# Pinning the first layer's TensorE instructions to program order, with other lengths of filler work in each step

## The chip, the cores and the metric

The kernel runs on one core of one Trainium2 chip. The time is device microseconds of one execution; a figure for a kernel is the median of its runs. The profile is of one execution. In it PE is TensorE (matmuls), PEld its weight loads, DVE is VectorE, ACT ScalarE, POOL GpSimd and SP SyncE; L100 is line 100 of the kernel before.

## What is computed

A trunk of two layers on x of shape (4, 512, 512), all in float32. The diff touches the first layer only. Cut to what matters:

```python
x  = L0_attn_hidden_states                  # (4, 512, 512)
xn = _layernorm(x)
x  = x + _L0_attn_ref(xn, ...) + _L0_ffn_ref(xn, ...)     # layer 0
xn = _layernorm(x)
x  = x + _L1_attn_ref(xn, ...) + _L1_ffn_ref(xn, ...)     # layer 1

# layer 0, attention: 32 heads of 16, a scan over NM = 32 mini-batches of K = 16 tokens
def step(carry, x):
    W1_s, b1_s = carry
    xq, xk, xv, eta_mb = x
    Z1 = xk @ W1_s + b1_s
    grad = _ln_fused_l2_bwd(Z1, xv - xk, ln_w, ln_b)
    Attn1 = jnp.tril(xq @ xk.swapaxes(-1, -2))
    b1_bar = b1_s - jnp.tril(eta_mb) @ grad
    Z1_bar = xq @ W1_s - eta_mb * Attn1 @ grad + b1_bar
    last_eta = eta_mb[:, :, -1, :, None]
    W1_new = W1_s - (last_eta * xk).swapaxes(-1, -2) @ grad
    b1_new = b1_s - jnp.sum(last_eta * grad, axis=-2, keepdims=True)
    out = xq + _ln(Z1_bar, ln_w, ln_b)
    return ((W1_new, b1_new), out)
# then: out = _ln(out, post_norm_weight, post_norm_bias) @ o_w.T

# layer 0, feed-forward: 512 -> 1408 -> 512
g = xf @ gate_w.T * gate_s;  u = xf @ up_w.T * up_s
out = (silu(g) * u) @ down_w.T * down_s
```

Every step of the scan needs the state that the step before it wrote, so the 32 steps come one after the other. The feed-forward part and the projections don't depend on the scan. Layer 1 is an attention with 16 heads and a feed-forward part with 4 experts.

## The kernel before

**Chunks.** Layer 0's 512 positions are cut into NCHUNK = 8 chunks of CH = 4 steps. A chunk has 4 batches of 64 tokens, CW = 256 columns.

**The step** (main loop of the scan, state in PSUM tiles `wacc`, `pz`, `pso`). `weights_out(n)` copies the state `wacc` to SBUF, as the block-diagonal operand `wq_bd` (DVE and ACT, L312) and as `wh` (ACT, L315). `first_product` is a matmul of 512 columns with `gsum` and 32 small matmuls `pz <- wq_bd, sk`. `queries_out` starts `pso` with 16 small matmuls from `wh`. `gradient` (L333 to L371) is a chain of vector operations on DVE with two on ACT, from `pz` to `grad`. `out_operands` makes `gh` (POOL, L401) and `a_bd` (DVE, L404). `update` copies `grad` into the block-diagonal `g_bd` (two copies on DVE, two on ACT, L375) and adds 16 small matmuls `wacc <- g_bd, km`; DVE adds to `gsum` (L386). `emit_out` adds 16 small matmuls to `pso` from `gh` and `a_bd` and DVE copies the result to `zch`; at the end of a chunk it is stored to DRAM and loaded back in another layout as `zb` (L434, L436). `prepare(n+1)` loads `kv` (L287) and makes `sk`, the second half of `wq_bd` and `km` on POOL (L294, L296, L301).

**The other work.** All that doesn't belong to the scan is written as Python generators that yield at certain points with a cost in microseconds. `between(ch)` chains them for a chunk: 11 slices of `gate_up` (8 matmuls of 256 columns into `pf`, with weights `wg`, `wu` loaded on SP; cost 3.43), the post-norm and output projection `finish(ch-1)` of the chunk that the scan has left, the `down` product into `pd`, a `value_bias` for layer 1, and what the next chunk of the scan needs: `norm_turn`, `keys`, `token_tile`, `queries`. `finish` runs, between its yields: a square on ACT (`pn_sq`, L543), two matmuls of 512 columns with `ones16`, for each a root on ACT and a reciprocal on DVE (`pn_rs`, L549 and L550), a product on DVE (L551), a scale and bias on ACT (L553) and an addition on POOL (L556), all on `zb`; then four matmuls of `onesd` and `zb`, a subtraction on DVE (L561) and a square on ACT (L562); then eight matmuls of one column, and for two halves four matmuls with `wo`, an update of `yf` on DVE (L576), a store, and a row norm; then transposes. Its first part is drawn in `between` behind the gate_up slice NI - 3 = 8, the others behind the parts of `down`. In the last chunk, finish(6) is drawn whole ahead of `down`.

**How they are mixed.** `fill(us)` draws from the chain of all generators until their costs have used up the time allowed; a debt is carried over in `due`. The main loop calls it three times in a step, with the three lengths of GAPS (L37): behind the step's gradient and operands, between `update` and `emit_out`, and behind `emit_out`. LAST_GAPS is for the last chunk, LAST_FINISH for the last finish.

**What sets the order on an engine.** The program is given to a scheduler[...]; it may move one past another where no dependency forbids it. `tc.keep_in_program_order` around an instruction holds it to the order in which the program issues it, among the instructions of its engine that are held so. Before, only three products at the end of layer 1 and the loads of its expert weights are held. Every matmul of layer 0 but a few goes through `mm` (L99); transposes are issued in `transposed` (L124) and `token_tile` (L234). `psum()` gives the PSUM tiles `pj`, of which there are two, as of `pf`.

## Time and profile before

| what | value |
|---|---|
| median of 3 runs | 2203.81 us (2200.7 to 2208.69) |
| the profiled execution's own time | 2204.35 us |
| its span in the profile | 2202.6 us |
| mean granted TensorE clock | 0.986 |
| layer 0 (to the last of its matmuls) | 0 to 1047 us |
| transition (PE waits for the load of `xe`) | 15.86 us |
| matmuls of one gate_up slice, PE | 3.45 us |
| pz with its gsum matmul; first half of pso; wacc; second half of pso, PE | 1.44; 1.19; 0.58; 0.61 us |
| one matmul into pd | 0.86 us |
| `pn_sq` pair; four `onesd <- zb`, PE | 1.98; 1.98 us |
| reciprocal of `pn_rs`, DVE | 3.35 us |
| addition to `zb`, POOL | 2.34 us |

A row of the timeline has the start in us from the start of the span, the duration, the engine, the line and operation, output and inputs with their shapes, how many instructions the row joins, and in brackets the idle time of the engine ahead of it with what ended it. Time that an engine is idle costs something only where that engine carries the work that sets the end.

### The profile page before, as it was taken

The numbers are of one execution on the slowest core, as the hardware profiler recorded it, in microseconds if no ns is written. First come the engines' busy times: TensorE is split into PE (matmuls) and PEld (weight loads), VectorE is DVE, ScalarE is ACT, GpSimd is POOL, SyncE is SP. The second block draws the span as 40 slices with busy tenths as digits, with TensorE's granted clock in tenths as the row PEclk, the third lists the DMA queues.
The fourth block names the chain that finished last, engine by engine and source line by source line (L and its number), as shares of the span: only waits on it lengthen the run. The fifth ranks groups of instructions, "written<-read, shape, count | busy, mean of one in ns | idle before, by whom it ended". The sixth has DMA issues, their size and how long they took to land.

```text
span 2202.6 us, 29431 instructions
## 1 busy us (share of the span) xinstructions
PE 2101.9 (95%) x10194; PEld 1195.0 (54%) x10194; DVE 1164.2 (53%) x2320; ACT 868.4 (39%) x1793; POOL 493.8 (22%) x540
## 2 busy tenths in 40 slices
PE   8999999999999999999799989999999999999999
PEld 6767586757667676745344444444444444444444
DVE  5445655455645554732011256666566656666663
ACT  2334353333433342423101255545454455455552
POOL 5232332233322332410010111111111111111110
PEclk9999999999999999999899889999999999999999
DMA  6555554546354556543830232333333323333332
GB/s 179 165 139 151 140 164 131 170 116 181 106 162 137 140 159 173 169 134 112 308 114 0 86 100 61 75 95 75 83 77 96 77 69 74 76 74 76 94 95 76
DMA packets 287856, 259.29 MB, mean 118 GB/s; under 512 B 52955, under 2 KB 210844, under 8 KB 286684
## 3 DMA queue, kind: packets, MB, share of 16 engines
q1 hardware_dynamic: 275296, 251.72, 40.8%
q10 hardware_dynamic: 11500, 5.32, 0.9%
q8 instruction: 82, 1.34, 0.3%
q14 instruction: 66, 0.54, 0.1%
q0 software_dynamic: 912, 0.36, 0.1%
HBM read 161.60 MB, written 29.62 MB: 87 GB/s over the span
## 4 chain that ended last, share of the span: by engine, by line
PE 75%; DVE 10%; ACT 8%; DMA 2%; issue 2%; POOL 1%; SPq 0%; ACTq 0%; DVEq 0%; POOLq 0%
PE pj L100 15%; PE pf L100 11%; PE po L1059 10%; PE pc L1044 7%; PE sc L998 5%; PE pd L100 5%; PE pq L989 5%; ACT prob L1003 3%; PE epg L845 3%; PE epo L890 2%; PE epu L845 2%; ACT prob L1005 2%; PE pso L100 2%; PE pz L100 2%; PE pk L982 2%
## 5 line engine op out<-in xcount | busy, mean ns | idle before, releaser
L998 PE MATMUL sc<-kT,qT 96*128 96x512 f32 x512 | 235.7, 598 | 15.1 <-ACT prob L1003 13.4
L975 POOL TENSOR_TENSOR kT<-t_k,t_k 32x512 f32<-32x512 f32 x64 | 80.7, 1261 | 722.0 <-PE pq L989 403.7
L1003 ACT ACTIVATE prob<-sc,mx 128x512 f32<-128x512 f32 x256 | 173.1, 683 | 146.5 <-DVE mx L1000 146.4
L1059 PE MATMUL po<-vo,ctxT 128*128 128x512 f32 x512 | 223.0, 592 | 1.5 <-ACT ctxT L1049 1.5
L1044 PE MATMUL pc<-prT,lv 128*128 128x512 f32 x496 | 224.1, 594 | 0.0
L1013 DVE STREAM_TRANSPOSE tt<-prob 128x512 f32<-128x512 f32 x252 | 166.6, 697 | 60.5 <-ACT prob L1005 58.2
L989 PE MATMUL pq<-cq,uq 128*128 128x512 f32 x384 | 175.2, 592 | 0.0
L100 PE MATMUL pf<-xT,wg 128*128 128x256 f32 x704 | 170.7, 384 | 3.5 <-DVE hid L456 1.9
L1005 ACT ACTIVATE prob<-prob,sm 128x512 f32<-128x512 f32 x256 | 171.7, 724 | 3.6 <-DVE sm L1004 3.6
L998 PEld LDWEIGHTS sc<-kT,qT 96*128 96x128 f32 x512 | 95.9, 190 | 140.9 <-issue 110.9
L1000 DVE TENSOR_REDUCE mx<-sc 128x1 f32<-128x512 f32 x256 | 164.3, 681 | 7.1 <-PE sc L998 4.5
L100 PE MATMUL pf<-xT,wu 128*128 128x256 f32 x704 | 166.9, 380 | 1.1 <-DMA wu<-in_wu 1.1
L100 PE MATMUL pd<-wd,hid 128*128 128x512 f32 x352 | 164.7, 601 | 0.2 <-DMA wd<-in_wd 0.2
L1059 PEld LDWEIGHTS po<-vo,ctxT 128*128 128x128 f32 x512 | 97.0, 190 | 124.2 <-issue 116.7
L1044 PEld LDWEIGHTS pc<-prT,lv 128*128 128x128 f32 x496 | 94.6, 191 | 120.1 <-issue 112.0
L100 PEld LDWEIGHTS pf<-xT,wg 128*128 128x128 f32 x704 | 130.9, 190 | 30.5 <-DVE hid L456 6.1
L100 PEld LDWEIGHTS pf<-xT,wu 128*128 128x128 f32 x704 | 133.4, 190 | 20.8 <-DMA wu<-in_wu 1.9
L1069 DVE TENSOR_TENSOR y<-po,y 128x512 f32<-128x512 f32 x64 | 44.2, 691 | 152.6 <-PE po L1059 152.6
L989 PEld LDWEIGHTS pq<-cq,uq 128*128 128x128 f32 x384 | 73.0, 190 | 91.8 <-issue 87.3
L983 ACT ACTIVATE kT<-pk,b_UK 64x512 f32<-64x512 f32 x64 | 43.7, 683 | 197.0 <-PE pk L982 197.0
L456 DVE SCALAR_TENSOR_TENSOR hid<-pf,us,sg 128x256 f32<-128x256 f32 x88 | 41.6, 476 | 122.3 <-ACT sg L455 121.6
L100 PEld LDWEIGHTS pd<-wd,hid 128*128 128x128 f32 x352 | 63.3, 190 | 60.4 <-issue 52.6
(253 smaller groups left out, 3145.4 us busy)
## 6 DMA issues: line engine op xcount, KB each, us to landing
prT<-tt SPq DMA_DIRECT2D x1008, 64.0 KB, 2.1
wd<-in_wd SPq DMA_DIRECT2D x176, 256.0 KB, 2.9
wg<-in_wg SPq DMA_DIRECT2D x88, 256.0 KB, 3.4
wu<-in_wu SPq DMA_DIRECT2D x88, 256.0 KB, 2.9
rows<-rows SPq DMA_DIRECT2D x128, 66.0 KB, 2.2
kv<-rows SPq DMA_DIRECT2D x32, 264.0 KB, 4.6
gu<-in_gu SPq DMA_DIRECT2D x4, 2048.0 KB, 8.0
xt<-in_x SPq DMA_DIRECT2D x32, 128.0 KB, 3.2
```

Source lines behind the costliest of these rows:

```text
L100: nc.tensor.matmul(out, lhsT=lhsT, rhs=rhs, start=start, stop=stop, skip_group_check=True)
L845: nc.tensor.matmul(ps, lhsT=w[:, c, col : col + P], rhs=xe[:, :, c, e, :], start=(c == 0), stop=(c == NC - 1))
L975: nc.gpsimd.tensor_sub(t[RD:mid, :], t1[RD:mid, :], t2[RD:mid, :])
L989: nc.tensor.matmul(pq, lhsT=w["uq"][i][:, h, :], rhs=cq[:, i, b, :], start=(i == 0), stop=(i == nq - 1))
L998: nc.tensor.matmul(ps, lhsT=qT[:KQ, i * P : (i + 1) * P], rhs=kT[:KQ, :], start=True, stop=True)
L1000: nc.vector.tensor_reduce(mx, ps, AX.X, ALU.max, negate=True)
L1003: nc.scalar.activation(pr, ps, AF.Exp, bias=mx, scale=1.0, accum_out=sm)
L1005: nc.scalar.mul(pr, pr, sm)
L1013: nc.vector.transpose(out=tt[:, :, :, i, :], in_=pr.rearrange("p (kb e j) -> p kb e j", e=2, j=K))
L1044: ins = nc.tensor.matmul(pc, lhsT=lv[:, b, k, :], rhs=prT[:, k, :], start=(k == 0), stop=(k == E - 1))
L1059: ins = nc.tensor.matmul(po[e], lhsT=ctxT[:, h, e * P : (e + 1) * P], rhs=w["vo"][:, h, :], start=(h == 0), stop=(h == HPG - 1),)
L1069: nc.vector.tensor_add(y[b][:, e, :], po.pop(e), y[b][:, e, :])
```

## The change

Two things. The three lengths of filler in each step become 13, 4 and 6 instead of 11, 4 and 8 (in the last chunk 12, 4, 3 instead of 10, 4, 5): the sum stays. And the TensorE instructions issued by `mm`, `transposed` and the key transposes of `token_tile` are held to program order. Behind these lines the line numbers grow by 2.

```diff
-GAPS, LAST_GAPS = (11.0, 4.0, 8.0), (10.0, 4.0, 5.0)
+GAPS, LAST_GAPS = (13.0, 4.0, 6.0), (12.0, 4.0, 3.0)
...
         def mm(out, lhsT, rhs, start=True, stop=True):
-            nc.tensor.matmul(out, lhsT=lhsT, rhs=rhs, start=start, stop=stop, skip_group_check=True)
+            tc.keep_in_program_order(
+                nc.tensor.matmul(out, lhsT=lhsT, rhs=rhs, start=start, stop=stop, skip_group_check=True)
+            )
...
         def transposed(src):
             pt = psum().rearrange("p (c t) -> p c t", c=NC)
             for c in range(NC):
-                nc.tensor.transpose(pt[:, c, :], src[:, c * P : (c + 1) * P], ident)
+                tc.keep_in_program_order(nc.tensor.transpose(pt[:, c, :], src[:, c * P : (c + 1) * P], ident))
             return pt
...
             pk = psum()
             for be in range(NC):
-                nc.tensor.transpose(pk[:, be * P : (be + 1) * P], k1[ch][:, be, tcols], ident)
+                tc.keep_in_program_order(nc.tensor.transpose(pk[:, be * P : (be + 1) * P], k1[ch][:, be, tcols], ident))
```

## The prediction

> **What bounds the kernel now.** I read the page's engine row first, then the windows, then the waits of TensorE, then the timeline around single waits.

> ```profile
> PE 2101.9 (95%) x10194; PEld 1195.0 (54%) x10194; DVE 1164.2 (53%) x2320; ACT 868.4 (39%) x1793; POOL 493.8 (22%) x540
> ```

> TensorE (PE) is busy 95% of the span, DVE only 53%. The second view cuts out layer 0's scan, and inside it the first finish (columns: stretch, its length, busy time and count of PE, PEld, DVE, ACT, POOL, granted clock, DMA share, GB/s):

> ```profile
> 98.00:1047.00 949.00, 907.62 (x6997) 628.78 (x6989) 498.42 (x1087) 345.80 (x692) 273.32 (x336) 0.99 0.51 147
> 185.00:215.00 30.00, 27.25 (x214) 19.03 (x213) 19.27 (x34) 18.18 (x28) 10.39 (x14) 0.95 0.46 141
> ```

> 949 us for 31 steps is about 30 us a step (28.4 where no transition lies in between), while the dependent loop is short: from pz to the end of the g_bd copies 9.7 to 10.4 us undisturbed, wacc 0.6, 3 to 5 until wq_bd and wh are rewritten, so about 14. The scan is bound by the amount of PE work. The change neither adds nor removes a matmul, so only PE's waits can be won or lost. PE rows of 0 to 1047 us have 50.9 us of gaps over 0.25 us, 10.4 of them before 98 us. The waits by releaser (total, times, longest):

> ```profile
> PE pz L100 <- POOL wq_bd L296: 6.7, 3, 2.2
> PE pj L100 <- ACT pn_sq L543: 5.5, 4, 2.9
> PE pj L100 <- POOL zb L556: 5.0, 5, 2.1
> PE pso L100 <- POOL gh L401: 4.6, 4, 2.0
> PE wacc L100 <- ACT g_bd L375: 4.3, 3, 1.7
> ```

> Two families: the steps' own products (pz, pso, wacc), and the post-norm of finished chunks (pn_sq, zb).

> **What the pinning removes.** The two instruction orders differ: PE has 1489 rows of grouped instructions before and 1469 after, because groups that the scheduler had split (six matmuls of emit_out, then wacc, then the other ten) become whole. After, each step is pz, pso, about 13 us of filler, wacc, filler of 4, emit_out, filler of 6. Layer 1's PE order is unchanged. The steps' badly placed products were waits like these:

> ```profile
> 270.55 0.37 PE L100 MATMUL pso<-a_bd,gh 128*32 128x68 f32 x10 [1.98 <-POOL gh L401]
> 407.35 1.08 PE L100 MATMUL pz<-wq_bd,sk 128*32 128x128 f32 x32 [2.22 <-POOL wq_bd L296]
> ```

> Summed from the gap rows: gh 1.99 + 1.66 + 0.40, wq_bd 3 x 2.22, g_bd 0.29 + 1.17 = **12.2 us**. With 13 us plus pz/pso (2.63: pz with gsum 1.44, pso 1.19) ahead of wacc, 15.6 us cover the 10-us gradient, and 6 us ahead of the next pz cover the 3 to 5 for wq_bd. I take all 12.2 as gone (bounds: 0 if other waits replace them at the same places, 12.2).

> **What the longer first gap does.** The fill times per step are the same in sum (23, in the last chunk 19), so no work moves between steps; about 2 us move from behind emit_out to ahead of wacc. That costs nothing itself: wacc has 4 + 6 us of filler behind it. Its cover ends where a finish stretches the gradient: pz to g_bd took 15.9, 18.3, 16.6 and 15 us in steps 13, 17, 21, 25, where the two 3.35-us reciprocals of finish lie on DVE. There 15.6 us don't suffice by 1 to 3 us: counted below.

> **What the pinning adds.** Filler matmuls are pinned too. What waits in finish, until now passed by later down or feature matmuls, now stops PE, and everything behind it: the next gate_up, wacc, pz. First finish, before:

> ```profile
> 190.37 0.81 ACT L375 COPY g_bd<-grad 32x256 f32<-32x256 f32 x2 [4.85 <-DVE grad L370]
> 191.20 1.06 ACT L543 ACTIVATE pn_sq<-zb 128x1024 f32<-128x1024 f32 x1
> 192.31 1.98 PE L100 MATMUL pj<-pn_sq,ones 128*128 128x512 f32 x4 [0.68 <-ACT pn_sq L543]
> ...
> 209.55 2.34 POOL L556 TENSOR_TENSOR zb<-zb,q 128x1024 f32<-128x1024 f32 x1
> 211.95 3.56 PE L100 MATMUL pj<-zb,onesd 128*128 128x256 f32 x8 [2.07 <-POOL zb L556]
> ```

> ACT's square stands behind step 4's g_bd copies in both orders, so it is ready 10.9 us after step 4's pz (181.4 to 192.3). After, the first gap of step 4 has one gate_up (3.45) ahead of the pn_sq matmuls: PE arrives at 2.63 + 3.45 = 6.1, and waits **4.8**. From pn_sq to the end of zb on POOL took 18 to 19.6 us in most finishes (19.6, 17.8, 17.2, 19.0, none read, 18.4, 15.5 for finish 0 to 6); I take 18.4. After has 14.7 us of PE work between: **3.6** of wait. Together 8.4 against 2.74 before.

> The other finishes in the same way, by the PE work that the new order puts between (17.3, 16.8, 16.1, 14.1, 14.7, 12.7): finish 1 to 3, own chain less filler 0.5 + 0.4 + 2.9 plus about 1.2 for pn_sq, 5.0 against 3.0; finish 4, 3.3 for the late wacc of step 21 and 1.5 for zb, 4.8 against 4.7; finish 5, 18.4 - 14.7, 3.8 against 0.6; finish 6, which the last chunk draws in one go with nothing between, zb 3.9 (2.8 by its own chain, 5.7 by 18.4; nearer its own row), the second pn_sq 3.6, transposes behind the row norm 2.4: 9.9 against 2.6; finish 7, 6.4 against 7.1. Sum 38.3 against 20.7: **+17.6**. Floor: the chain's durations alone add to about 14 us (so +7); ceiling: every chain 19.6 and pn_sq always at 10.9 (so +30).

> Smaller: start-up 12.6 against 10.4 (the transposes of k and the bias chain no longer overtaken by gate_up) +2.2; the bo_part pairs of value_bias 6.9 against 4.8, +2.1; rest 1.6 against 2.7, -1.1. DMA: the same transfers on SP; weight loads are issued in the changed order but a buffer ahead, as before; wg's wait is in the rest.

> Sum without the clock: -12.2 + 17.6 + 2.2 + 2.1 - 1.1 = **+8.6 us**.

> [...]Fewer but longer gaps also touch TensorE's clock. Behind the 2.07-us gap above, the eight matmuls took 3.56 us where the same two fours take 1.98 elsewhere: +1.6, with 0.95 granted in 185 to 215. Gaps of 2.88 (at 987) and 2.69 (at 1036) cost +1.3 and +1.5, while 2.22-us gaps at 407, 527 and 650 cost nothing (clock 1.00). The long one shows the full price:

> ```profile
> 1062.55 5.16 PE L845 MATMUL epg<-xe,gu 128*128 128x512 f32 x8 [15.86 <-DMA xe<-xe_d]
> 1067.54 3.60 PE L845 MATMUL epu<-xe,gu 128*128 128x512 f32 x8
> ```

> 5.16 - 3.60 = 1.56. [...]here the trace decides that gaps of 2 to 3 us may do. [...]By the trace, seven or eight of about 3 us or more give about 11.5, less before's four (1.6 + 1.3 + 1.5, and 1.2 behind gaps of 1.72 and 0.56 at 697 to 700; 5.6): +6. I take **+4**, since three gaps of 2.2 show that one near the edge isn't sure to slow anything.

> 2204.35 (profiled execution; its span is 2202.6, and 1.75 around it stays) + 8.6 + 4 = **2217 us**, 0.6% more. It stands 0.5 above the median of 2203.81, well within the runs' 2200.7 to 2208.7.

> **Rivals.** *A, the other side: the finishes are covered.* If ACT's square runs ahead of step 4's gradient (zb had landed at 184.6, 3.2 after pz) and POOL adds zb at once, the 17.6 shrinks to about zero, the other +3.2 remains, the 12.2 is won, and with shorter gaps two of before's slow spells (1.5 each) go: 2204.35 - 12.2 + 3.2 - 3 = 2192. For it: the floor of 14 us for the chain is below most fillers. Against: the ACT order of after still has g_bd's copies first, and before's chains never came below 15.5. It decides if the pn_sq wait is under 1 us and the chain under 15.

> *B, even trade.* Chains near 16 us and gaps too short to lower the clock: +8.6 becomes about 0, 2204 within 6. For it: three gaps of 2.22 left the clock alone. Against: pn_sq's 4.8 doesn't depend on the chain.

> *C, doubled stalls.* A PE that stops in finish delays the next gradient, whose DVE work then meets the next reciprocals, and wacc and pz wait as well: finish's +17.6 becomes +30 (ceiling), the clock +10, 2204 - 12 + 3 + 30 + 10 = 2235 to 2240. For it: steps 13 to 25 with 15 to 18 us chains. Against: a late PE gives DVE time to catch up[...].

> That nothing changes is excluded by the order.

> **How the numbers follow.** The forecast, new waits in finish that outweigh the 12.2 saved, has 0.58, with its own range 2209 to 2227; A 0.18; B 0.14; C 0.10. About 0.3% (6.6 us, 2197.2 to 2210.4) is what a measurement tells from no change. A gives faster 0.18; B, mostly inside, with the forecast's low edge left out, same 0.14; the rest slower 0.68. The range for eight in ten runs from A's upper half, 2197, to C's lower half, 2236.

> **What would show it.** Right: no PE wait over 1 us on gh or wq_bd; wacc waits only in finish's steps; a PE gap of 4 to 5 us before the first pn_sq, and of 3 to 4 before zb in finish 0, 5 and 6; the granted clock in those stretches at or under 0.95; layer 1, from the transition on, within 2 us. Wrong: pn_sq and zb waits that sum below before's 10.5; PE gaps of the scan below 50.9; or a longer time with the gaps unchanged, which would be matmuls that got slower, a cause I count at nothing.

## The result: slower, and the profile after

The changed kernel takes 2306.16 us (median of 4 runs, 2302.42 to 2309.01) against 2205.59 of the kernel before beside it: ratio 1.046, 95% interval 1.0436 to 1.0483, some 100 us more where the prediction had 13. The profiled execution has a span of 2305.5 us (2202.6 before). First the engine row of its page, then the stretch of the scan that the prediction showed of before (columns as there):

```profile
PE 2136.5 (93%) x10194; PEld 1209.1 (52%) x10194; DVE 1159.4 (50%) x2320; ACT 867.7 (38%) x1793; POOL 492.3 (21%) x540
```

```profile
98.00:1047.00 949.00, 853.07 (x6699) 597.11 (x6699) 473.75 (x1048) 321.24 (x608) 268.15 (x333) 0.95 0.47 134
```

Same 10194 matmuls, but in the same 949 us only 6699 of them were done instead of 6997, PE was busy 54.6 us less, and the granted clock was 0.95 instead of 0.99. The waits of PE in the first 1140 us (what it waited for: us in total, times, longest):

```profile
PE pd L101 <- DMA wd<-in_wd: 38.4, 7, 7.9
PE pj L101 <- POOL zb L558: 17.5, 5, 5.1
PE pf L101 <- DVE hid L458: 14.4, 6, 4.0
PE pj L101 <- ACT pn_sq L545: 9.4, 3, 5.0
PE wacc L101 <- DVE g_bd L377: 5.3, 2, 4.7
```

The waits for gh and wq_bd are gone, as the change wants. In their place stand zb and pn_sq, as forecast, and two that the prediction does not have at all: the down product `pd` waiting for its weights `wd`, and gate_up (`pf`) waiting for `hid`, which frees its PSUM tile.

I added up PE's idle stretches over 0.25 us in both traces, up to the transition to layer 1, sorted by place:

| place | before, us | after, us | difference |
|---|---|---|---|
| the steps' own products (gh, wq_bd, g_bd outside finish) | 12.2 | 0 | -12.2 |
| last wd loads of `down`, chunks 1 to 7 | 0 | 38.4 | +38.4 |
| finish 0 to 7 (pn_sq, zb, hid, g_bd, yf, row norm) | 20.7 | 58.8 | +38.1 |
| start-up | 10.4 | 13.6 | +3.2 |
| value_bias and the rest | 7.5 | 6.6 | -0.9 |
| sum (rounded) | 50.7 | 117.4 | +66.7 |
| matmuls of layer 0, end of layer 0 less the gaps | 996.0 | 1025.0 | +29.0 |
| transition, wait for `xe` | 15.9 | 17.3 | +1.4 |
| layer 1 to the end of the span | 1140.0 | 1145.8 | +5.8 |

Together they are the 102.9 us between the two spans. Layer 1 has the same PE order in both; its 5.8 us lie in what it varies by (1138.5 to 1146.6 us in the profiles of this study).

**The wait for wd.** Here is chunk 2 in the timeline of the changed kernel; SPq rows are DMA issues of SyncE:

```profile
394.03 1.10 PE L101 MATMUL pd<-wd,hid 128*128 128x512 f32 x2
394.72 1.25 SPq L276 DMA_DIRECT2D rows<-rows  x3
396.01 2.33 SPq L276 DMA_DIRECT2D rows<-rows  x5
398.44 0.85 SPq L469 DMA_DIRECT2D wd<-in_wd  x2
...
401.64 3.78 PE L101 MATMUL pd<-wd,hid 128*128 128x512 f32 x4 [6.51 <-DMA wd<-in_wd]
```

The last two wd loads of the chunk are issued by SP behind the second eight of the 16 stores of `rows` that a chunk has. These eight can only start when the token tile's last product (`lrw`, just ahead of 394) has been through DVE and ACT, and they take 3.6 us to issue. PE then waits for the load to land. Now the same place in the kernel before:

```profile
373.26 1.10 PE L100 MATMUL pd<-wd,hid 128*128 128x512 f32 x2
373.95 3.64 SPq L274 DMA_DIRECT2D rows<-rows  x8
374.21 0.59 PE L100 MATMUL pz<-gsum,bones 128*128 128x256 f32 x2
...
377.69 1.93 SPq L467 DMA_DIRECT2D wd<-in_wd  x2
378.76 1.89 PE L100 MATMUL pf<-xT,wu 128*128 128x256 f32 x8
380.49 1.89 PE L100 MATMUL pf<-xT,wg 128*128 128x256 f32 x8
...
387.39 1.88 PE L100 MATMUL pd<-wd,hid 128*128 128x512 f32 x4
```

SP's order is the same: wd late, behind the stores. But PE does not stand there. It runs the next step's pz and pso and two gate_up slices of the next chunk and takes up `pd` at 387, some 8 us after the loads were issued. That lateness was always there; the free order covered it. This holds for chunks 2, 3 and 4, where the last two wd loads stand behind all 16 stores in both traces (21.6 of the 38.4 us). In chunks 1 and 5 (10.1 us) the kernel before has no wd load behind the stores; there the pinning also moved one. In chunk 6 (6.3 us) it has one behind them, the changed kernel two.

**The wait for hid.** ACT in the changed kernel, in the step of finish 2:

```profile
449.06 0.81 ACT L377 COPY g_bd<-grad 32x256 f32<-32x256 f32 x2 [4.85 <-DVE grad L372]
449.89 1.06 ACT L545 ACTIVATE pn_sq<-zb 128x1024 f32<-128x1024 f32 x1
...
452.26 0.84 ACT L457 ACTIVATE sg<-pf,gs 128x256 f32<-128x256 f32 x2
```

ACT is idle for 4.85 us until DVE ends the gradient, with the silus of two finished gate_up slices queued behind the g_bd copies. With both `pf` tiles full PE stops for 3.83 us. In the same finish before, ACT has the square and two silus ahead of the copies:

```profile
410.83 1.04 ACT L543 ACTIVATE pn_sq<-zb 128x1024 f32<-128x1024 f32 x1
...
414.64 0.47 ACT L455 ACTIVATE sg<-pf,gs 128x256 f32<-128x256 f32 x1
416.82 0.47 ACT L455 ACTIVATE sg<-pf,gs 128x256 f32<-128x256 f32 x1 [1.70 <-PE pf L100]
418.20 0.81 ACT L375 COPY g_bd<-grad 32x256 f32<-32x256 f32 x2 [0.91 <-DVE grad L370]
```

So holding TensorE's order moved silus on ACT; e1 below, with the pinning alone, has such waits of up to 4.0 us too. Why the scheduler puts them there is not seen in a trace; that it does is.

### The profile page after: what moved, and what is told of

Same layout as the page of the kernel before. It is cut to its first block, busy times and chain, and to the rows that moved or that the text cites. A ratio compares the mean times of both kernels' runs of the same rounds, so it can differ in the third digit from the quotient of the medians.

```text
span 2305.5 us, 29473 instructions
## 1 busy us (share of the span) xinstructions
PE 2136.5 (93%) x10194; PEld 1209.1 (52%) x10194; DVE 1159.4 (50%) x2320; ACT 867.7 (38%) x1793; POOL 492.3 (21%) x540
## 4 chain that ended last, share of the span: by engine, by line
PE 72%; DVE 12%; ACT 10%; DMA 3%; issue 2%; SPq 1%; POOL 0%; ACTq 0%; DVEq 0%; POOLq 0%
PE pj L101 14%; PE pf L101 11%; PE po L1061 10%; PE pc L1046 6%; PE pd L101 6%; PE pq L991 5%; PE sc L1000 5%; ACT prob L1005 3%; PE epg L847 3%; ACT prob L1007 2%; PE epo L892 2%; PE epu L847 2%; PE pz L101 2%; PE pso L101 2%; PE pk L984 2%
## 5 line engine op out<-in xcount | busy, mean ns | idle before, releaser
L101 PE MATMUL pd<-wd,hid 128*128 128x512 f32 x352 | 172.5, 628 | 39.3 <-DMA wd<-in_wd 38.4
L101 PE MATMUL pf<-xT,wg 128*128 128x256 f32 x704 | 177.0, 396 | 15.9 <-DVE hid L458 14.4
```

The costliest lines, as they stand in the source:

```text
L101: nc.tensor.matmul(out, lhsT=lhsT, rhs=rhs, start=start, stop=stop, skip_group_check=True)
```

## Experiments

All ratios are to the kernel before, run beside each.

| run | what differs | median, us | ratio (95%) |
|---|---|---|---|
| e1 | pinning, old lengths | 2314.46 | 1.0504 (1.0477 to 1.0531) |
| e2 | new lengths, nothing pinned | 2204.76 | 0.9995 (0.9982 to 1.0009) |
| e3 | stores of rows one part later | 2283.72 | 1.0366 (1.0343 to 1.0389) |
| e4 | finish not pinned | 2307.95 | 1.0482 (1.0451 to 1.0512) |
| e5 | stores of rows on ACT's queue | 2319.36 | 1.0523 (1.0488 to 1.0559) |
| e6 | only the scan's products pinned | 2191.28 | 0.9948 (0.9923 to 0.9972) |
| e7 | only the filler pinned | 2283.11 | 1.0356 (1.0331 to 1.0380) |
| e8 | useless matmuls ahead of the last pd | 2335.24 | 1.0594 (1.0570 to 1.0618) |
| e9 | all pinned but gate_up and down | 2189.23 | 0.9931 (0.9916 to 0.9947) |
| e10 | scan, gate_up and down pinned | 2289.14 | 1.0385 (1.0369 to 1.0401) |
| e11 | stores of rows behind value_bias | 2265.02 | 1.0275 (1.0257 to 1.0294) |
| e12 | ACT's g_bd copies on POOL | 2298.28 | 1.0431 (1.0410 to 1.0452) |
| e13 | e9 with the old lengths | 2197.23 | 0.9966 (0.9953 to 0.9978) |
| e14 | useless matmuls in the wd waits | 2297.55 | 1.0426 (1.0410 to 1.0442) |

### Which half of the change: e1 and e2

e1 is the changed kernel with the first line of the diff taken back; e2 is the kernel before with that line alone.

> The pinning alone, with the old filler lengths 11, 4, 8. Theory P (the pinning makes the 100 us: PE stops at the last wd load of each chunk, at finish, and the clock falls behind each stop): 2285 to 2315 us, seven waits of pd for wd of 4 to 8 us still there. Rival G (the longer first gap makes it): within 10 us of before, about 2205.

> The new filler lengths 13, 4, 6 alone, nothing pinned. Theory P: 2195 to 2215 us, no wait of pd for wd over 1 us. Rival G: 2250 or more.

The pinning is the whole loss: 1.0504 alone, while the lengths alone are within the noise. In e1 the wacc waits for g_bd grow to 17.9 us (7.6 after), so the longer first gap seems to help a pinned kernel; its median is 8 us above the changed kernel's, but the two intervals overlap.

### Which pinned work: e4, e6, e7, e9, e10

In each, some matmuls go through an `mf` that is `mm` without the pin:

```diff
+        def mf(out, lhsT, rhs, start=True, stop=True):
+            nc.tensor.matmul(out, lhsT=lhsT, rhs=rhs, start=start, stop=stop, skip_group_check=True)
...
-                    mm(pf[:, j, :], w[:, c, :], xTs[ch][:, c, :], c == 0, c == NC - 1)
+                    mf(pf[:, j, :], w[:, c, :], xTs[ch][:, c, :], c == 0, c == NC - 1)
...
-                mm(pd, hid[ch][:, i, u * P : (u + 1) * P], w, i == 0, i == NI - 1)
+                mf(pd, hid[ch][:, i, u * P : (u + 1) * P], w, i == 0, i == NI - 1)
```

This is e9. e4 frees finish, e6 all that isn't the scan's, e7 only the scan's products; e10 frees all but the scan's, gate_up and down.

> The changed kernel with the matmuls and transposes of finish not pinned. Theory F (finish's place in PE's order makes its stops): PE's gaps at finish fall from about 59 to about 21 us, and some ten slow spells go: 2245 to 2265 us. Rival A (the stops come from the orders of ACT and DVE, where silu and square stand behind the step's g_bd copies, whatever PE's order): within 15 us of 2306.

Nothing gained, but neither theory was tested: in layer 0 the orders of PE and of ACT in e4's trace are those of the changed kernel, instruction for instruction by their names. The scheduler left finish where it was, with the gate_up, down and scan matmuls around it held. So pn_sq and zb wait the same 9.4 and 17.5 us, and the 1.8 us between the two medians are noise.

> Lengths 13, 4, 6, and only the scan's own products (pz, pso, wacc, emit_out) pinned; all filler (gate_up, down, features, token tiles, finish, value_bias, latents, transposes) free. Theory L (it is the pinned filler that [...]moves stores and silus): about as before, 2195 to 2212 us. Rival M (pinning the step products alone does it): 2280 or more.

> The counterpart: lengths 13, 4, 6, all filler pinned, the scan's own products free. Theory L: 2285 to 2315 us, wd waits of 30 us or more. Rival M: 2195 to 2215.

The filler's pinning is the loss. e6 is even 0.5% faster than before (its interval lies below 1), a little under the time expected. e7 loses as much time as Theory L said, to 2 us, but not by the wd waits that it named. The stop changes its name: the wd waits go, but pso waits 32.3 us for gh, seven times, up to 8.8. At 264 us, for one, PE has pz and the first half of pso, and right behind them the second half, which needs the gradient: no filler lies between. Which filler:

> Lengths 13, 4, 6; everything pinned as in the changed kernel except gate_up and down (pf, pd), which are free. Theory L (PE needs a stock of matmuls that may pass a waiting one; the feed-forward part is that stock): 2190 to 2215 us, no wait for wd over 2 us, PE gaps of layer 0 under 60 us. Rival N (any pinned filler stops PE at finish and token tiles): 2240 or more.

> The counterpart: gate_up, down and the scan's products pinned, all the rest (features, token tiles, finish, value_bias, transposes, latents) free. Theory L: 2285 to 2312 us, as the changed kernel, with wd waits of 30 us or more, since SP's order is the changed kernel's. Rival N: 2190 to 2225.

Clear-cut: gate_up and down free, all else pinned, gives 2189.23, the lowest median (e6's interval overlaps with it), just under the range expected; the two of them pinned and the rest free keeps most of the loss, at 2289.14. There the wd waits are 26.3 us, below the 30 expected. Here are PE's two largest waits of layer 0 in e9:

```profile
PE pj L101 <- POOL zb L561: 4.6, 6, 1.2
PE pj L101 <- DMA wob<-in_W_O: 4.3, 5, 1.6
```

wd is down to 0.5 us and hid to 0.7; zb falls from 17.5 to 4.6 although finish itself is pinned. PE's gaps in layer 0 are 35.1 us, against 50.7 before and 117.4 after. In chunks 2 to 4 SP still issues the last two wd loads behind 16 stores, and PE no longer waits: it is the free matmuls that cover them. In chunks 1 and 5 the load that the pinning had moved behind the stores is ahead of them again.

### The place of the stores on SP: e3, e5, e11

e3 and e11 collect the stores of a token tile in a list and issue them later, on SP as before:

```diff
-            for b2 in range(2):
-                for i in range(CH):
...
-                    nc.sync.dma_start(
-                        out=rows_d[ch][i, :, :, 2 * u + b2, :].rearrange("s t x -> t s x"), in_=t[p0 : p0 + K]
-                    )
+            pend.append((ch, u, t))
+            if ch == 0:
+                flush()
...
             yield from extra
+            flush()
```

e11 flushes behind value_bias (`extra`) as shown, e3 behind each `take(dn, 1)`; e5 leaves the place and writes `nc.scalar.dma_start`.

> The changed kernel with the stores of rows issued behind the down part that follows, on the same queue (SP), so that the last wd load of a chunk no longer stands behind all 16 of them. Theory Q (that load's place in SP's order is what PE waits for): the waits of pd for wd fall from 38 us to under 10, six slow spells of 1.5 us go with them, 2255 to 2272 us. Rival S (the load is only the last of several things that late; another wait takes its place): within 15 us of 2306.

Between the two ranges: the wd waits went, but PE now waited 21.6 us for `wob`, four times up to 6.8, the load behind the stores in chunks 1 to 4. In chunks 5 to 7, which have no value_bias, the wait vanished.

> The changed kernel with all 16 stores of rows of a chunk issued behind value_bias, on SP as before. In SP's order only 1 to 4 of them still stand ahead of wd and wob. Theory Q (place behind 16 stores): waits for wd and wob together under 10 us (38 and 2 in the changed kernel), 2250 to 2275 us. Rival S (the wait moves on to kv, rows or something else behind SP): above 2285.

With one to five stores ahead of wd and wob instead of 16, the two wait 0.5 and 1.4 us, and 41 us are gone, as Theory Q said. Part came back as S had it: PE waits 12.7 us for `wg`; the longest, 7.4, is for a load that SP issues behind the four `z` stores of the chunk's end, at 549 us, when PE had been idle since 546.

> The changed kernel with the 128 stores of rows on ACT's queue instead of SP's. Theory Q (16 stores in a row on SP, 7 to 8 us of issue, hold up whatever load stands behind them: wd in the changed kernel, wob in the run before): no wait of PE for wd or wob over 2 us, 35 to 40 us of gaps less, 2250 to 2270 us. Rival X (the stores only move the trouble to ACT, where they stand ahead of silu and of the gradient's root): the wd waits go, the hid and wacc waits grow by as much, above 2285.

Rival X was right in the main: wacc's waits grow, though those for hid do not (12.1 us). On ACT the DMA issues stood among the copies; here the second copy of g_bd started 4.66 us after the engine's last work, behind eight of them:

```profile
137.75 9.68 ACTq L276 DMA_DIRECT2D rows<-rows  x8
...
147.74 0.40 ACT L377 COPY g_bd<-grad 32x256 f32<-32x256 f32 x1
147.74 5.01 ACTq L276 DMA_DIRECT2D rows<-rows  x8
152.80 0.40 ACT L377 COPY g_bd<-grad 32x256 f32<-32x256 f32 x1 [4.66 <-DMA rows<-rows]
```

wacc waits 7.6 us for that copy, 17.7 us in all. The issues themselves add to 3.1 and 3.2 us in these two rows, as on SP (3.3); the rest of the 9.68 and 5.01 us is time in which ACT's queue stood between two issues.

### What stands ahead on ACT: e12

```diff
-            (nc.vector.tensor_copy if be < 2 else nc.scalar.copy)(g_bd[r, :, be, :], g[r])
+            (nc.vector if be < 2 else nc.gpsimd).tensor_copy(g_bd[r, :, be, :], g[r])
```

> The changed kernel with the two copies of grad into g_bd that ACT makes given to POOL, so that silu and the square of pn_sq no longer stand behind the gradient on ACT. Theory H (head of line on ACT): the first wait for pn_sq (5.0 us) goes, the three waits for hid of 3.8 to 4.0 us fall to about 1.3 (DVE is busy with the gradient until then), 13 us of gaps and some 6 us of clock: 2282 to 2292 us. Rival V (DVE's order holds hid back just as long, POOL delays gh): within 8 us of 2306.

The waits move as Theory H says, the sum doesn't: the first pn_sq wait is gone, and hid falls from 14.4 to 6.2 us, its three long waits from about 3.9 to 1.4 or 1.5. But POOL is late with its copies: wacc waits 13.2 us for them, up to 7.2. The median is 8 us lower, just where Rival V's range ends, and the two intervals overlap.

### The clock: e8 and e14

```diff
+                if u == 1 and i == {1: 10, 2: 9, 3: 9, 4: 9, 5: 10, 6: 9}.get(ch):
+                    for _ in range(6):
+                        mm(pd, ident, nought.to_broadcast([P, HS]), False, False)
                 mm(pd, hid[ch][:, i, u * P : (u + 1) * P], w, i == 0, i == NI - 1)
```

> The changed kernel with six extra matmuls of 512 columns, with a factor of zero added into pd, ahead of the last pd matmul of each of seven chunks, that is in the middle of its wait for wd (5.1 us of PE work where 4.5 to 7.9 us were idle). Theory C (each long gap costs about 1.5 us of clock behind it, on top of itself): 36 us of work more, yet 6 to 11 us faster than the changed kernel, 2295 to 2300 us, and a granted clock of 0.95 or more from 262 to 300 and 530 to 560. Rival D (the clock's loss hangs on the chunk's traffic, not on the gap): 0 to 4 us slower than the changed kernel, clock there unchanged at 0.83 to 0.91.

e8 has `ch > 0 and i == NI - 1` in the first line. In four of its seven chunks the wait is ahead of i = 9, not of the last i = 10, so the extra work came behind the stop, and the seventh chunk has hardly a wait (0.4 us). It cost 29 of its 36 us. Its time tells nothing of the clock, but its trace does: in chunk 1, where the extra work did fill the stop, the clock from 262 to 300 rose from 0.91 to 1.00, and from 385 to 420 and 530 to 560, where the stops stayed, it remained 0.85 and 0.83.

> The changed kernel with six extra matmuls of 512 columns, with a factor of zero added into pd, right ahead of the matmul that waits for wd in six chunks (the ninth or tenth of its part), so 5.1 us of PE work where 4.5 to 7.9 us were idle. Theory C (the matmuls behind a long stop are slowed by its idling, about 2 us for each): 31 us of work more, yet 8 to 14 us faster than the changed kernel, 2292 to 2299 us, and a granted clock of 0.95 or more from 262 to 300, 385 to 420 and 530 to 560 (0.91, 0.85, 0.83 before). Rival D (the clock's loss hangs on the chunk's work or traffic, not on the stop): 0 to 4 us slower than the changed kernel, the clock there unchanged.

The windows around three of the filled stops, first of the changed kernel, then of e14; the clock is the third number from the end:

```profile
262.00:300.00 38.00, 32.04 (x232) 21.12 (x231) 19.39 (x46) 9.74 (x22) 11.80 (x14) 0.91 0.58 159
385.00:420.00 35.00, 27.65 (x202) 15.01 (x201) 11.40 (x29) 6.89 (x18) 6.14 (x6) 0.85 0.61 165
530.00:560.00 30.00, 20.79 (x126) 12.44 (x126) 15.21 (x35) 7.92 (x15) 8.52 (x9) 0.83 0.56 160
```

```profile
262.00:300.00 38.00, 35.11 (x243) 22.73 (x242) 19.67 (x48) 9.62 (x21) 11.47 (x14) 1.00 0.57 161
385.00:420.00 35.00, 31.16 (x218) 17.12 (x218) 11.36 (x30) 8.42 (x20) 7.35 (x8) 1.00 0.61 175
530.00:560.00 30.00, 24.89 (x136) 14.69 (x126) 14.61 (x34) 8.52 (x15) 8.96 (x11) 0.94 0.56 160
```

With the stop filled and nearly the same DMA share (0.57 instead of 0.58; 0.61 and 0.56 in both), the granted clock rises from 0.91, 0.85 and 0.83 to 1.00, 1.00 and 0.94; in the third window 2.9 us of the stop are left. In these windows the clock went with the idling, not with the traffic. In the time the effect is not shown. The median is 8.6 us below the changed kernel's, inside C's range, but the two intervals overlap; and the profiled execution of e14 was itself 8 us above its median, with a lower clock at other stops (0.85 instead of 0.92 from 185 to 230) and only 1.9 us less of matmul time besides the 31 us added.

```profile
208.80:212.21 3.41, 1.34 (x4) 0.51 (x4) 1.80 (x5) 1.82 (x3) 3.41 (x3) 1.00 0.27 80
212.21:215.63 3.42, 3.42 (x9) 2.72 (x9) 0.01 (x1) 0.00 (x0) 1.20 (x4) 0.50 0.00 0
403.36:406.77 3.41, 1.77 (x9) 1.21 (x7) 0.71 (x2) 0.94 (x3) 1.09 (x3) 1.00 0.00 0
406.77:410.19 3.42, 2.84 (x67) 2.70 (x68) 1.61 (x5) 0.42 (x1) 2.03 (x4) 1.00 0.00 0
```

PE's busy time is the first figure behind the comma, the clock the third from the end. The four `pd` matmuls at 401.64 us of the changed kernel, shown above, lie in a stretch at half clock and took 3.78 us; the four at 387.39 of the kernel before, at full clock, took 1.88, half as long. PE is busy for 16.6 us in the half-clock stretches of layer 0 before and for 73.5 us after. If half of that is what the clock cost, an estimate from these rows, it is 8.3 and 36.7 us; the difference, 28.4 us, is close to the 29.0 us by which the matmuls of layer 0 grew.

### The lengths once more: e13

> The run e9 (gate_up and down free, all else pinned) with the old lengths 11, 4, 8. Theory P (the lengths do nothing by themselves; it is the order of the step's own products that wins): within 4 us of e9's 2189. Rival G2 (9.2 + 2 us of cover are too few where finish stretches the gradient, waits of wacc for g_bd come back): 2196 to 2206 us, with 5 to 12 us more of PE waits for g_bd.

The lengths are worth about 8 us in the good version (0.9966 against 0.9931; the intervals just don't meet), which theory P didn't expect. G2's number came true, but not its reason: waits for g_bd rise by 1.0 us only, from 3.4 to 4.4. PE's gaps grow by 4.5 us, in several small places (the largest is hid, 2.1 more); the rest of the difference of the two profiles, 4.2 us, lies in layer 1, where the code is the same. So the lengths seem to help, and how much of the 8 us is theirs stays open.

## Why the prediction was wrong, point by point

The prediction had +8.6 us of waits, +4 of clock and nothing for the rest; measured are +66.7, +29.0 and, for the transition and layer 1, +7.2.

- **"I take all 12.2 as gone"** was right: the changed trace has no PE wait for gh or wq_bd left. e6 and e9, which keep the scan pinned and free the feed-forward part, are 12 to 14 us faster than before. That this is the same number is in part chance: in e9 the waits for gh, wq_bd and g_bd fall by 8.5 us (15.9 to 7.4), and other gaps by 7.0.
- **"DMA: ... weight loads are issued in the changed order but a buffer ahead, as before"** is the step that failed most: it put at nothing what became 38.4 us. A buffer ahead was no cover where up to 16 stores that waited for PE's own latest product stood ahead of the load. SP's order could be read off before the run, and in chunks 2 to 4 needed no change to do harm; what had to be asked was what PE does between 373 and 387 us in the trace of before, and whether it may still do it. The prediction asked that of finish alone.
- **"What the pinning adds ... +17.6"** had the right mechanism for pn_sq and zb and left others out: 38.1. The wait for the first pn_sq came nearly as computed (4.8 forecast, 4.97 measured), as did zb's first (3.6 and 3.94). In the first two small errors cancel: the 10.9 us run from the small products of pz (181.4) and PE's 6.1 from its gsum matmul (180.9), and PE took 6.4. Finish 0 and 5 to 7 together had 28.5 forecast and about 31.6 measured; the miss is in finish 1 to 4, 9.8 against about 27. Left out were the silus: the prediction looked for ACT's square behind g_bd, but not for the gate_up slices whose silus would stand behind it too (hid, three waits of 3.8 to 4.0), nor all of the g_bd waits (2.3 in finish 3 and 4.7 in finish 4; 3.3 forecast for the second alone). The ceiling given, +30, was below the truth as well, because it held only finish's own chain.
- **The clock, "I take +4"**, had the right cause and was mis-sized: the matmuls of layer 0 took 29 us more. Per stop, the estimate from the rows (about 1.5 us) was a little low: over nine kernels with long stops (the changed one, e1, e3 to e5, e7, e10 to e12), the excess of matmul time over before, divided by the stops over 2 us that they have more than before, is 1.9 to 2.9 us (29.0 by 15 in the changed kernel). The count was what failed: 7 or 8 stops of about 3 us or more forecast, 16 of over 3 us found, 20 of over 2.5. The pieces above show how two gaps of about 2 us differed. Each of the three 2.22-us gaps of before, which cost nothing, was split by a boundary and left 1.77 us of work or more in each of its pieces: the luck of where they fell.
- **Rival C** had the right side and was too small, for it multiplied finish instead of adding places. **Rival A**, the covered finish at 2192, is near what e9 reached, but by another way: it took a stock of matmuls free to pass a waiting one, not a shorter chain.
- **"That costs nothing itself"** of the lengths: right for the kernel as it was (e2, 0.9995).
- **"Layer 1 ... within 2 us"**: it was 5.8 us longer, with the same PE order, inside what it varies by from run to run.

## What to carry to other kernels

Pin the instructions whose order matters, and leave a stock of independent work free to pass them: in these runs an engine that could not run past a waiting matmul turned late loads and activations into stops (38.4 us of waits for wd and 14.4 for hid in the changed kernel), and pinning it also rearranged the queues of ACT and, in places, of SP. Before pinning, go through the trace of before for loads and copies that are late but unnoticed, and name what the engine runs meanwhile; if the pin forbids that, add the lateness to the sum. A version that pins the scan, the features and finish but leaves gate_up and down free is faster than both kernels, 0.9931 of the time before; with the scan alone pinned it is 0.9948, which these runs don't tell apart.

## What the hardware showed beyond that

Issuing took time on the queue's engine: eight small stores of `rows` took 3.6 to 5.1 us of SP. When ACT issued them, the two groups shown held its queue for 5.0 and 9.7 us, with an activation or a copy held up behind them. And the stops of PE cost more than their length: 66.7 us of additional idling in layer 0 came with 29 us of slower matmuls, and the granted clock rose from 0.85 and 0.91 to 1.00 where useless matmuls filled a stop. Which stops had a slow stretch behind them went with where they fell: in layer 0 of both traces a piece of 3.413 us at full clock was followed by one at half clock in all 20 cases with less than 1.4 us of work in it, and in none of 561 with more than 2.0 us.
